# A two-layer centroid convolution on one core: alternating logits rounds with numerators and denominators, a reordered head, and centring on GpSimd

## The chip, the cores and the metric

The kernel runs on one core of a Trainium2 chip. The metric is the device time of one execution in microseconds. The program was run several times and the median is given; one more execution was profiled, and every view of the profile comes from that one. Engines are named as the profile names them: PE is TensorE's matmuls, PEld its weight loads, DVE is VectorE, ACT is ScalarE, POOL is GpSimd, SP is the queue of SyncE that issues most DMAs. "SPq" in a view is SP's queue.

## The reference

The input x has 16 images of 256 channels with 28 x 28 pixels, float32. The output is `x + f(gn(x))`, where `gn` normalizes each of 32 groups of 8 channels over its group and its pixels, and `f` is

```python
out = amm_conv3x3(v, centroids1, wsub1)      # v = gn(x)
out = relu(bn1(out))
out = amm_conv3x3(out, centroids2, wsub2)
out = bn2(out)
out = se_layer(out)                          # mean over pixels, two small layers, sigmoid gate
return relu(out + v)

def amm_conv3x3(x, centroids, w_sub):        # centroids [C, 16, 9], w_sub [C, 9, 256]
    p = 3x3 patches of x                     # per channel and pixel, 9 taps
    d = squared distance of p to each of the channel's 16 centroids
    attn = softmax(-d)                       # over the 16 centroids
    lut = centroids @ w_sub                  # per channel, [16, 256]
    return sum over channels and centroids of attn * lut
```

As `lut = centroids @ w_sub`, the result of a layer is also a product of `w_sub` with the softmax-weighted mean of the centroids, nine numbers per channel and pixel, and this is how the kernel computes it. The square of p is the same for all centroids of a channel and drops out of the softmax.

## The kernel before

**Tiles.** A layer of an image is cut into four blocks: half of the input channels (`hh`, 128 channels) by half of the pixels (`t`, 14 rows, N = 392 pixels), in the order `BLOCKS = ((0, 0), (0, 1), (1, 1), (1, 0))`. For each block the kernel

- gathers the nine taps of each channel from a padded image in HBM into a patch tile `pt` (`patches`, six DMAs for each half p of the block, issue lines L335 and L339; the source is called `home`);
- multiplies them by the centroids: `logits` (L349) of four groups mm = 0 to 3, each of 32 channels. One round of a group is 16 matmuls on 32 x 32 tiles of the array into four PSUM banks; two halves p = 0 (mm 0, 1) and p = 1 (mm 2, 3) take one patch tile each;
- takes exponentials of the four banks on ScalarE (`exps`, L361) into `e`;
- computes the ninth numerator and the denominators, summed over all four groups (`num_b`, L410, two banks "nb"), splits and joins them on ScalarE and VectorE (`split_b` L421 and L423, `join_b` L430 and L433), and takes the reciprocal (L436);
- computes the other numerators (`num_a`, L396, two banks "na" per group). Groups 0 and 1 are copied out by ScalarE (`copy_a`, L464) and multiplied by the reciprocal on GpSimd (`scale_q`, L459); groups 2 and 3 are multiplied on VectorE as they leave PSUM (`scale_a`, L470). `spread` (L447, L451) brings the reciprocals to the right partitions.

The fp32 matmuls take two passes, so that one round of logits shows as 32 matmul instructions.

**Products.** The four blocks of an image form a 2 x 2 by 2 x 2 product with `w_sub`, done with seven products in place of eight; sums of operands are made on GpSimd (`mix`, L485 and L487). Each product is nine matmuls on the full array (`product`, L478, into a bank "acc"), and VectorE and ScalarE put the results together (`acc_copy`, `acc_add` L515, `norm_out` L533).

**Layer 2, hh = 0.** These blocks are "wide": the logits of mm = 0 may be too large for a plain exponential. They are copied (`wide_copy`, L367), turned and their maximum taken on VectorE (`wide_turn`, L372 and L375), the maximum subtracted on GpSimd (`wide_sub`, L381), turned back (`wide_back`, L385) and only then exponentiated (`wide_exp`, L389).

**Order.** The order of work is written out by hand. `at(cluster, sub, function, ...)` files a step under a cluster number and a position inside it; at the end all steps are emitted sorted by (cluster, sub), and every engine, and SP's queue of DMAs, runs its instructions in the order of emission. An image takes eight clusters, a block two: in cluster g (even) its mm 0 and 1 go, in g + 1 (odd) mm 2 and 3; in cluster g + 2 its denominators and the numerators of mm 0 and 1, in g + 3 the numerators of mm 2 and 3. So an even cluster holds on TensorE: two rounds of logits, `num_b` and two `num_a` of the block before, and a product; an odd cluster two rounds of logits, two `num_a` and a product. Images start every eight clusters, layer 2 follows layer 1 at cluster 128; 256 clusters carry logits.

**PSUM.** All banks come from one ring of eight (`p_ring`), which hands a freed bank to the next request. A round of logits takes four, `num_b` two, a `num_a` two, a product one.

**Patches.** There are two patch tiles (`NPT = 2`), so the patches for cluster c + 2 can be issued only when the logits of cluster c have read the tile. `patches` stands at position 0.5 of cluster c, and the staging loads for layer 2's weights at position 0.6.

**Weights of layer 2.** During clusters 8 to 80 the kernel ranks input channels of layer 2 and reorders its weights accordingly: loads into a staging tile (`h0_load` L633, `codes_load` L641, `sub_load` L651), scatters to HBM by GpSimd's DMAs, and then centring: `prep_wd2` squares a third of the centroid table (`center_sq`, L251), `prep_wd3` has TensorE sum the squares (`center_add`, L256) and adds them, `prep_wd4` subtracts means and stores. The staging tile is single.

**Head.** Before the first cluster the first image is normalized (`gn_stats`, `gn_mean`, `gn_var`, `gn_apply` for its two channel halves), written to HBM, the patch tiles are set to one, and the centroid tables of layer 1 are centred.

Of the kernel before, what the change touches and what calls it, by code (L numbers as in the profile page):

```python
# [17 lines left out]
P = 128  # L18
# [7 lines left out]
K = 16  # L26
# [10 lines left out]
NPT = 2  # L37
# [30 lines left out]
def kernel(  # L68
# [20 lines left out]
    nc = tc.nc  # L89
    B, C, _ = x.shape  # L90
    NB = C // P
# [115 lines left out]
    kbias = kst[:, 16:48]  # L207
# [40 lines left out]

    def center_sq(wf, c0, w):
        sq = rpool.tile([P, N], F32, tag="r", name="sq")  # L250
        nc.vector.tensor_mul(sq[:, :w], wf[:, c0 : c0 + w], wf[:, c0 : c0 + w])  # L251
        return sq
# [5 lines left out]

    def center_mean(wf, n):
        g = wf.rearrange("p (g k) -> p g k", k=K)  # L260
        nc.vector.tensor_reduce(cst[:, : n // K], g, axis=AX.X, op=ALU.add)
        nc.vector.tensor_scalar_mul(cst[:, : n // K], cst[:, : n // K], 1.0 / K)
        nc.vector.tensor_sub(g, g, cst[:, : n // K].unsqueeze(2).to_broadcast([P, n // K, K]))

# [410 lines left out]
    def prep_wd2(part):  # L675
        pw["sq"] = center_sq(pw["st"][:, 512:1536], 384 * part, min(384, 1024 - 384 * part))

# [3 lines left out]
    def prep_wd4():  # L681
        st = pw.pop("st")
        center_mean(st[:, 512:1536], 1024)
        f = st[:, 512:1536].rearrange("p (g n) -> p g n", n=32)
        nc.vector.tensor_sub(f, f, kbias.unsqueeze(1).to_broadcast([P, 32, 32]))
        nc.sync.dma_start(d_wd[1], st[:, 512:1536])
# [147 lines left out]
    def at(cl, sub, f, *a, **kw):  # L834
        jobs.setdefault((cl, sub), []).append((f, a, kw))
# [20 lines left out]
    for j, u in enumerate(blocks):  # L856
        g = 2 * j
        u["w"] = j
        wide = u["l"] == 1 and u["hh"] == 0
        for p in range(2):  # L860
            u["pt", p] = pts[p]
            at(g + p - NPT, 0.5, patches, u, p, nc.gpsimd if g + p < 5 else None)
            for q in range(2):
                mm = 2 * p + q
                at(g + p, 0.1 + 0.1 * q, logits, u, mm)
                if wide and mm == 0:
                    at(g, 0.12, wide_copy, u, mm)
                    at(g, 0.9, wide_turn, u, mm)
                    at(g, 0.95, wide_sub, u, mm)
                    at(g + 1, 0.3, wide_back, u, mm)  # L870
                    at(g + 1, 0.9, wide_exp, u, mm)
                else:
                    at(g + p, 0.12 + 0.1 * q, exps, u, mm)
        at(g + 2, 1.3, num_b, u)
        at(g + 2, 1.4, split_b, u)
        at(g + 2, 1.5, join_b, u)
        at(g + 2, 1.6, recip_dve, u)
        at(g + 2, 1.7, spread, u, 4)
        at(g + 2, 1.71, scale_q, u, 4)
        for mm in range(2):  # L880
            at(g + 2, 1.35, num_a, u, mm)
            at(g + 2, 1.45, copy_a, u, mm)
            at(g + 3, 1.8, spread, u, mm)
            at(g + 3, 1.8, scale_q, u, mm)
        for mm in range(2, 4):
            at(*((g + 2, 1.8) if mm == 2 else (g + 3, 0.05)), spread, u, mm)
            at(g + 3, 1.0, num_a, u, mm)
            at(g + 3, 1.1, scale_a, u, mm)

    for l in range(2):  # L890
        for b in range(B):
# [3 lines left out]
            for c, (w, r, ks) in PRODUCTS.items():  # L895
                at(g + c, 2.0, product, (n, c), us[r], w, ks)
            for mm in (4, 2, 3, 0, 1):
# [4 lines left out]
            c11, c12, c21, c22 = (0, 0), (0, 1), (1, 0), (1, 1)  # L902
            at(g + 6, 0.0, acc_copy, l, b, c11, (n, 5))
            at(g + 7, 0.0, acc_copy, l, b, None, (n, 6))
# [13 lines left out]
            if l == 0:  # L918
# [8 lines left out]
                if b + 1 < B:  # L927
                    at(g + (-1 if b else 2), 2.6, load_x, b + 1)
                    for q in range(NB):
                        at(g + (1 + 2 * q if b else 4), 0.3, gn_stats, b + 1, q)  # L930
                    at(g + 4, 1.05 if b else 1.96, gn_mean, b + 1)
                    at(g + 4, 1.33 if b else 1.97, gn_var, b + 1)
                    for q in range(NB):
                        at(g + 5, 0.9, gn_apply, b + 1, q)
                        at(g + 5, 1.9, to_home1, b + 1, q)
            else:
# [18 lines left out]

    at(1, 0.6, load_w, 0, "A11")
    at(3, 0.6, load_w, 0, "S3")
    at(3, 0.6, load_w, 0, "A22")
    at(6, 0.6, load_w, 0, "A12")
# [23 lines left out]
    for part in range(3):  # L983
        at(43 + 2 * part, 1.9, prep_wd2, part)
        at(44 + 2 * part, 1.05, prep_wd3, part)
    at(51, 0.3, prep_wd4)
    at(52, 0.6, prep_cw0)
# [18 lines left out]

    for k in range(NB):
        gn_stats(0, k)
        gn_mean(0, k, 1)
        gn_var(0, k, 1)  # L1010
        gn_apply(0, k)
        if k == 0:
            for i in range(2):
                to_home1(0, 0, i)
            nc.vector.memset(pts[0], 1.0)
            nc.gpsimd.memset(pts[1], 1.0)
    for hh in range(2):
        center(wts["wd", hh].rearrange("p a b c -> p (a b c)"), 512)
    at(-0.5, 0.7, to_home1, 0, 1)
    at(0, 1.95, setup_bn)  # L1020
    for t in hpads:
# [159 lines left out]
```

## Time and profile before

| | value |
|---|---|
| median of 3 runs | 2773.7 us (2772.71 to 2774.86) |
| the profiled execution | 2760.28 us |
| its span, first to last instruction | 2758.7 us |
| mean granted clock of TensorE | 0.987 |
| PE busy | 2674.9 us (97%) |
| PEld busy | 1297.7 us (47%) |
| DVE busy | 1732.6 us (63%) |
| ACT busy | 1454.4 us (53%) |
| POOL busy | 2066.8 us (75%) |

A row of the timeline or of the groups reads: start, busy time, engine, line, operation, output tile <- input tiles, shape, number of instructions, and in brackets the engine's idle time before it with the tile and line that released it. In the row of slices each digit is the busy share of a fortieth of the span in tenths. A row of the waits names who waited, for whom, the total in us, how often, and the longest. The profiled execution is 13.4 us shorter than the median of the timed runs, so sums made on the profile are carried over as differences.

### The profile page before, as it was taken

The page shows a single profiled execution, that of the slowest core. Times are in us where ns is not written, and L with a number is a line of the kernel's source. Part 1 is how long each engine was busy: PE and PEld are TensorE (multiplying, and loading weights), DVE is VectorE, ACT ScalarE, POOL GpSimd, SP SyncE. Part 2 cuts the span into 40 slices and gives each one's busy share as a digit, 9 for nine tenths or more (in the row PEclk, how much of TensorE's full clock was granted, in tenths as well). Part 3 has the DMA queues.
Part 4 walks back from the last instruction along what each step waited for, and adds up shares of the span by engine and source line. Part 5 has one row for each costly group of instructions (what it writes and reads, how often), then busy time and mean ns, then how long its engine had stood idle before and what let it go on. Part 6 is the DMA issues. An engine that isn't in the chain of part 4 may idle for free. (4 is left out here: it accounts for less than half of the span.)

```text
span 2758.7 us, 87946 instructions
## 1 busy us (share of the span) xinstructions
PE 2674.9 (97%) x37076; PEld 1297.7 (47%) x37076; DVE 1732.6 (63%) x3950; ACT 1454.4 (53%) x3277; POOL 2066.8 (75%) x1420
## 2 busy tenths in 40 slices
PE   5989999799999999999999999999999999999997
PEld 2444444344444444444444444444444444444443
DVE  5765555765555565565576766676766666766664
ACT  4444455445455445455455466656566656556653
POOL 4756787738877767766678777888877788877787
PEclk9999999999999999999999999999999999999998
DMA  9665677546677656666585455445555545555541
GB/s 202 149 135 136 165 191 184 146 107 158 154 189 189 157 128 151 158 160 150 117 183 122 105 123 122 111 104 114 114 123 123 115 104 113 116 117 123 117 105 47
DMA packets 223025, 374.51 MB, mean 136 GB/s; under 512 B 30152, under 2 KB 193336, under 8 KB 222624
## 3 DMA queue, kind: packets, MB, share of 16 engines
q1 hardware_dynamic: 215392, 334.50, 53.8%
q0 software_dynamic: 7232, 34.30, 3.6%
q8 instruction: 296, 4.85, 0.8%
q14 instruction: 105, 0.86, 0.1%
HBM read 288.91 MB, written 79.80 MB: 134 GB/s over the span
## 5 line engine op out<-in xcount | busy, mean ns | idle before, releaser
L361 ACT ACTIVATE e<-lg 128x392 f32<-128x392 f32 x1920 | 777.7, 530 | 822.7 <-PE lg L349 821.7
L487 POOL TENSOR_TENSOR qp<-qp,qp 128x784 f32<-128x784 f32 x512 | 938.2, 1862 | 41.8 <-DVE qp L470 41.8
L478 PE MATMUL acc<-qp,w_S 128*128 128x392 f32 x2048 | 709.0, 497 | 5.3 <-POOL qp L487 5.2
L459 POOL TENSOR_TENSOR qp<-qp,rb 128x784 f32<-128x784 f32 x256 | 473.0, 1869 | 253.6 <-DVE rb L451 253.6
L349 PE MATMUL lg<-pt,wd 32*32 32x392 f32 x16384 | 533.5, 503 | 28.8 <-DVE half_sum L515 17.3
L451 DVE STREAM_SHUFFLE rb<-r 128x392 f32<-128x392 f32 x1024 | 550.8, 605 | 0.0
L478 PEld LDWEIGHTS acc<-qp,w_S 128*128 128x128 f32 x2048 | 388.5, 191 | 296.7 <-POOL qp L487 10.9
L478 PE MATMUL acc<-qp,w_A 128*128 128x392 f32 x1536 | 521.3, 493 | 0.0
L396 PE MATMUL na<-e,cwa 64*32 64x392 f32 x8192 | 412.1, 498 | 10.0 <-issue 9.8
L430 DVE SCALAR_TENSOR_TENSOR r<-nb,kst,r 128x392 f32<-128x392 f32 x128 | 79.8, 624 | 517.5 <-ACT r L421 510.6
L478 PEld LDWEIGHTS acc<-qp,w_A 128*128 128x128 f32 x1536 | 292.5, 190 | 213.1
L410 PE MATMUL nb<-e,cwb 64*32 64x392 f32 x8192 | 372.2, 497 | 0.0
L349 PEld LDWEIGHTS lg<-pt,wd 32*32 32x32 f32 x16384 | 230.9, 103 | 282.8 <-issue 179.6
L436 DVE RECIPROCAL r<-r 128x392 f32<-128x392 f32 x128 | 331.9, 2593 | 0.0
L459 POOL TENSOR_TENSOR qo<-qo,rb 128x392 f32<-128x392 f32 x128 | 131.1, 1024 | 220.3 <-DVE rb L447 220.2
L470 DVE TENSOR_TENSOR qp<-na,rb 128x392 f32<-128x392 f32 x512 | 252.4, 555 | 56.1 <-PE na L396 53.1
L396 PEld LDWEIGHTS na<-e,cwa 64*32 64x32 f32 x8192 | 145.2, 106 | 234.6 <-ACT e L361 123.5
L410 PEld LDWEIGHTS nb<-e,cwb 64*32 64x32 f32 x8192 | 146.2, 107 | 209.2 <-issue 126.5
L464 ACT COPY qp<-na 128x392 f32<-128x392 f32 x512 | 211.8, 512 | 10.9 <-PE na L396 10.8
L421 ACT ACTIVATE r<-nb,kst 128x392 f32<-128x392 f32 x128 | 87.5, 684 | 102.3 <-PE nb L410 99.8
L367 ACT COPY e<-lg 128x392 f32<-128x392 f32 x128 | 52.9, 500 | 152.9 <-PE lg L349 152.9
L485 POOL TENSOR_TENSOR qo<-qo,qo 128x392 f32<-128x392 f32 x128 | 130.8, 1022 | 2.2
(143 smaller groups left out, 1778.1 us busy)
## 6 DMA issues: line engine op xcount, KB each, us to landing
pt<-home SPq DMA_DIRECT2D x768, 209.0 KB
pt<-home SPq DMA_DIRECT2D x753, 104.5 KB
home<-xpad SPq DMA_DIRECT2D x31, 899.0 KB
xt<-in_x SPq DMA_DIRECT2D x30, 784.0 KB
out_dram<-y SPq DMA_DIRECT2D x32, 392.0 KB
w_S<-d_wS SPq DMA_DIRECT2D x4, 576.0 KB
st<-in_wsub SPq DMA_DIRECT2D x4, 512.0 KB
st<-d_wa SPq DMA_DIRECT2D x16, 128.0 KB
```

Source lines behind the costliest of these rows:

```text
L349: nc.tensor.matmul(bk[32 * c : 32 * c + 32, :N].rearrange("p (r w) -> p r w", w=W), lhsT=wts["wd", u["hh"]][32 * i : 32 * i + 32, mm, c, : ...
L361: nc.scalar.activation(eg[:, i, :], bk[:, :N], AF.Exp, scale=2.0)
L396: nc.tensor.matmul(bs[r][32 * i : 32 * i + 32, :N], lhsT=wts["cwa", u["hh"]][64 * r : 64 * r + 64, mm, i, :], rhs=es[64 * r : 64 * r + 64, ...
L410: nc.tensor.matmul(bs[r][32 * i : 32 * i + 32, :N], lhsT=wts["cwb", u["hh"]][64 * r : 64 * r + 64, mm, i, :], rhs=es[64 * r : 64 * r + 64, ...
L436: nc.vector.reciprocal(u["r"], u["r"])
L451: nc.vector.stream_shuffle(rb[:, r, :], u["r"], mask_of(2 * mm + r))
L459: nc.gpsimd.tensor_tensor(q, q, u.pop(("rb", mm)), ALU.mult)
L464: nc.scalar.copy(u["q", 2 * mm + r], bk[:, :N])
L470: nc.vector.tensor_mul(u["q", 2 * mm + r], bk[:, :N], rb[:, r, :])
L478: nc.tensor.matmul(accs[key][:, :N], lhsT=wl[w][:, k, :], rhs=us["q", k], start=first and n == 0, stop=last and n == len(ks) - 1,)
L485: nc.gpsimd.tensor_tensor(out_u["q", 8], in0["q", 8], in1["q", 8], ALU.subtract)
L487: nc.gpsimd.tensor_tensor(pair(out_u, mm), pair(in0, mm), pair(in1, mm), ALU.subtract)
```

## The change

The change has four parts.

1. **Rounds.** In an even cluster the second round of logits (mm 1) goes from position 0.2 to 1.32, behind `num_b`, and its `exps` to 1.42, behind `split_b`; the two `num_a` go to 1.45, so that `join_b` at 1.5 is emitted behind them. In an odd cluster the second round (mm 3) goes to 1.12, behind the numerators of mm 2, and the numerators of mm 3 to 1.2.
2. **Patches.** All patch DMAs go from 0.5 to 1.6 of their cluster, and so behind the loads that stand at 0.6 and ahead of those at 1.65 and later.
3. **Centring of layer 2.** The squares (`prep_wd2`), the subtraction of the means and that of `kbias` (`prep_wd4`) go from VectorE to GpSimd, and `prep_wd4` from position 0.3 to 1.9 of cluster 51.
4. **Head.** The patch tile is set to one in two pieces; the first centroid table is centred between the normalizations of the two channel halves, the second one in cluster 0; some loads and the work on the second image get other positions; the first image's first product is made in cluster 4 in place of 5.

```diff
--- before.py
+++ after.py
@@ -246,9 +246,9 @@
 
     cst = const.tile([P, 64], F32, name="cst")
 
-    def center_sq(wf, c0, w):
+    def center_sq(wf, c0, w, eng=None):
         sq = rpool.tile([P, N], F32, tag="r", name="sq")
-        nc.vector.tensor_mul(sq[:, :w], wf[:, c0 : c0 + w], wf[:, c0 : c0 + w])
+        (eng or nc.vector).tensor_mul(sq[:, :w], wf[:, c0 : c0 + w], wf[:, c0 : c0 + w])
         return sq
 
     def center_add(wf, c0, w, sq):
@@ -256,11 +256,11 @@
         nc.tensor.matmul(ps[:, :w], lhsT=nhalf_sb, rhs=sq[:, :w], start=True, stop=True)
         nc.vector.tensor_add(wf[:, c0 : c0 + w], wf[:, c0 : c0 + w], ps[:, :w])
 
-    def center_mean(wf, n):
+    def center_mean(wf, n, eng=None):
         g = wf.rearrange("p (g k) -> p g k", k=K)
         nc.vector.tensor_reduce(cst[:, : n // K], g, axis=AX.X, op=ALU.add)
         nc.vector.tensor_scalar_mul(cst[:, : n // K], cst[:, : n // K], 1.0 / K)
-        nc.vector.tensor_sub(g, g, cst[:, : n // K].unsqueeze(2).to_broadcast([P, n // K, K]))
+        (eng or nc.vector).tensor_sub(g, g, cst[:, : n // K].unsqueeze(2).to_broadcast([P, n // K, K]))
 
     def center(wf, n):
         for c0 in range(0, n, 256):
@@ -673,16 +673,16 @@
             )
 
     def prep_wd2(part):
-        pw["sq"] = center_sq(pw["st"][:, 512:1536], 384 * part, min(384, 1024 - 384 * part))
+        pw["sq"] = center_sq(pw["st"][:, 512:1536], 384 * part, min(384, 1024 - 384 * part), nc.gpsimd)
 
     def prep_wd3(part):
         center_add(pw["st"][:, 512:1536], 384 * part, min(384, 1024 - 384 * part), pw["sq"])
 
     def prep_wd4():
         st = pw.pop("st")
-        center_mean(st[:, 512:1536], 1024)
+        center_mean(st[:, 512:1536], 1024, nc.gpsimd)
         f = st[:, 512:1536].rearrange("p (g n) -> p g n", n=32)
-        nc.vector.tensor_sub(f, f, kbias.unsqueeze(1).to_broadcast([P, 32, 32]))
+        nc.gpsimd.tensor_sub(f, f, kbias.unsqueeze(1).to_broadcast([P, 32, 32]))
         nc.sync.dma_start(d_wd[1], st[:, 512:1536])
 
     def prep_cw0():
@@ -859,10 +859,10 @@
         wide = u["l"] == 1 and u["hh"] == 0
         for p in range(2):
             u["pt", p] = pts[p]
-            at(g + p - NPT, 0.5, patches, u, p, nc.gpsimd if g + p < 5 else None)
+            at(g + p - NPT, 1.6, patches, u, p, nc.gpsimd if g + p < 5 else None)
             for q in range(2):
                 mm = 2 * p + q
-                at(g + p, 0.1 + 0.1 * q, logits, u, mm)
+                at(g + p, (0.1, (1.32, 1.12)[p])[q], logits, u, mm)
                 if wide and mm == 0:
                     at(g, 0.12, wide_copy, u, mm)
                     at(g, 0.9, wide_turn, u, mm)
@@ -870,7 +870,7 @@
                     at(g + 1, 0.3, wide_back, u, mm)
                     at(g + 1, 0.9, wide_exp, u, mm)
                 else:
-                    at(g + p, 0.12 + 0.1 * q, exps, u, mm)
+                    at(g + p, (0.12, (1.42, 1.14)[p])[q], exps, u, mm)
         at(g + 2, 1.3, num_b, u)
         at(g + 2, 1.4, split_b, u)
         at(g + 2, 1.5, join_b, u)
@@ -878,14 +878,14 @@
         at(g + 2, 1.7, spread, u, 4)
         at(g + 2, 1.71, scale_q, u, 4)
         for mm in range(2):
-            at(g + 2, 1.35, num_a, u, mm)
-            at(g + 2, 1.45, copy_a, u, mm)
+            at(g + 2, 1.45, num_a, u, mm)
+            at(g + 2, 1.46, copy_a, u, mm)
             at(g + 3, 1.8, spread, u, mm)
             at(g + 3, 1.8, scale_q, u, mm)
         for mm in range(2, 4):
             at(*((g + 2, 1.8) if mm == 2 else (g + 3, 0.05)), spread, u, mm)
-            at(g + 3, 1.0, num_a, u, mm)
-            at(g + 3, 1.1, scale_a, u, mm)
+            at(g + 3, 1.0 if mm == 2 else 1.2, num_a, u, mm)
+            at(g + 3, 1.1 if mm == 2 else 1.25, scale_a, u, mm)
 
     for l in range(2):
         for b in range(B):
@@ -893,14 +893,14 @@
             g = 8 * n
             us = blocks[4 * n : 4 * n + 4]
             for c, (w, r, ks) in PRODUCTS.items():
-                at(g + c, 2.0, product, (n, c), us[r], w, ks)
+                at(g + c - (c == 5 and n == 0), 2.0, product, (n, c), us[r], w, ks)
             for mm in (4, 2, 3, 0, 1):
                 at(g + 5, 2.5, mix, us[0], mm, us[1], us[0])
                 at(g + 7, 2.5 if mm < 2 else 1.75, mix, us[1], mm, us[2], us[1])
                 at(*((g + 7, 2.6) if n < B - 1 else (g + 8, 1.0)), mix, us[0], mm, us[2], us[0])
                 at(g + 10, 1.0, mix, us[0], mm, us[0], us[3])
             c11, c12, c21, c22 = (0, 0), (0, 1), (1, 0), (1, 1)
-            at(g + 6, 0.0, acc_copy, l, b, c11, (n, 5))
+            at(g + (6 if n else 5), 0.0, acc_copy, l, b, c11, (n, 5))
             at(g + 7, 0.0, acc_copy, l, b, None, (n, 6))
             at(g + 8, 0.0, acc_add, l, b, None, (n, 7))
             at(g + 9, 0.0, acc_add, l, b, c21, (n, 8), c11)
@@ -925,14 +925,14 @@
                         for r in range(2):
                             at(g + 12 + o + (o and r), (0.5, 2.9)[r] if o == 0 else (2.4, 2.9)[r], to_home2, b, o, r)
                 if b + 1 < B:
-                    at(g + (-1 if b else 2), 2.6, load_x, b + 1)
+                    at(*((g - 1, 2.6) if b else (2, 1.65)), load_x, b + 1)
                     for q in range(NB):
                         at(g + (1 + 2 * q if b else 4), 0.3, gn_stats, b + 1, q)
-                    at(g + 4, 1.05 if b else 1.96, gn_mean, b + 1)
-                    at(g + 4, 1.33 if b else 1.97, gn_var, b + 1)
+                    at(g + 4, 1.05 if b else 2.1, gn_mean, b + 1)
+                    at(g + 4, 1.33 if b else 2.2, gn_var, b + 1)
                     for q in range(NB):
-                        at(g + 5, 0.9, gn_apply, b + 1, q)
-                        at(g + 5, 1.9, to_home1, b + 1, q)
+                        at(g + 5, 0.9 if b else 0.3, gn_apply, b + 1, q)
+                        at(g + 5, 1.9 if b or q else 0.9, to_home1, b + 1, q)
             else:
                 last = b == B - 1
                 at(*((g + 11, 0.6) if last else (g + 13, 2.6)), load_x, b, last)
@@ -953,9 +953,9 @@
                     at(g + 11, 0.95, flags)
                     at(g + 12, 2.9, flag_sum)
 
-    at(1, 0.6, load_w, 0, "A11")
-    at(3, 0.6, load_w, 0, "S3")
-    at(3, 0.6, load_w, 0, "A22")
+    at(1, 1.65, load_w, 0, "A11")
+    at(3, 1.65, load_w, 0, "S3")
+    at(3, 1.65, load_w, 0, "A22")
     at(6, 0.6, load_w, 0, "A12")
     for c, m in ((5, "S1"), (7, "S2"), (8, "S4"), (6, "S3")):
         at(c, 1.96, combine, m)
@@ -983,7 +983,7 @@
     for part in range(3):
         at(43 + 2 * part, 1.9, prep_wd2, part)
         at(44 + 2 * part, 1.05, prep_wd3, part)
-    at(51, 0.3, prep_wd4)
+    at(51, 1.9, prep_wd4)
     at(52, 0.6, prep_cw0)
     at(53, 1.9, prep_cwa)
     for part in range(4):
@@ -1004,20 +1004,26 @@
     at(g + 4, 0.6, load_w, 1, "A12")
     at(g + 5, 0.6, load_w, 1, "A22")
 
-    for k in range(NB):
+    def norm0(k):
         gn_stats(0, k)
         gn_mean(0, k, 1)
         gn_var(0, k, 1)
         gn_apply(0, k)
-        if k == 0:
-            for i in range(2):
-                to_home1(0, 0, i)
-            nc.vector.memset(pts[0], 1.0)
-            nc.gpsimd.memset(pts[1], 1.0)
-    for hh in range(2):
+
+    def center_wd(hh):
         center(wts["wd", hh].rearrange("p a b c -> p (a b c)"), 512)
+
+    nc.vector.memset(pts[0][:, :4], 1.0)
+    norm0(0)
+    for i in range(2):
+        to_home1(0, 0, i)
+    nc.vector.memset(pts[0][:, 4:], 1.0)
+    nc.gpsimd.memset(pts[1], 1.0)
+    center_wd(0)
+    norm0(1)
+    at(0, 1.95, center_wd, 1)
     at(-0.5, 0.7, to_home1, 0, 1)
-    at(0, 1.95, setup_bn)
+    at(0, 1.96, setup_bn)
     for t in hpads:
         at(1, 1.95, nc.gpsimd.memset, t, 0.0)
```

## The prediction

> **What bounds the kernel now.** I read the busy row first, then the slices, then TensorE's busy time in stretches.
>
> ```profile
> PE 2674.9 (97%) x37076; PEld 1297.7 (47%) x37076; DVE 1732.6 (63%) x3950; ACT 1454.4 (53%) x3277; POOL 2066.8 (75%) x1420
> PE   5989999799999999999999999999999999999997
> 2006.30:2088.70 82.40, 82.40 (x1179) 40.35 (x1192) 55.54 (x120) 48.90 (x112) 66.84 (x41) 1.00 0.51 115
> ```
>
> TensorE sets the time, with about 84 us of idle, nearly all before 800 us and in the tail. The third line is one layer-2 image (start:end, length, then PE, PEld, DVE, ACT, POOL, clock, DMA): no gap. A TensorE wait added to a cluster is thus lost in full; a gain must shorten TensorE's own runs. The timeline shows them (start, length):
>
> ```profile
> 2006.30 2.03 PE L349 MATMUL lg<-pt,wd 32*32 32x392 f32 x64
> 2008.25 2.86 PE L410 MATMUL nb<-e,cwb 64*32 64x392 f32 x64
> 2010.91 1.52 PE L396 MATMUL na<-e,cwa 64*32 64x392 f32 x32
> 2012.37 0.93 PE L478 MATMUL acc<-qo,w_A 128*128 128x392 f32 x2
> 2018.49 2.02 PE L349 MATMUL lg<-pt,wd 32*32 32x392 f32 x64
> 2020.44 1.64 PE L396 MATMUL na<-e,cwa 64*32 64x392 f32 x32
> 2022.01 0.93 PE L478 MATMUL acc<-qo,w_A 128*128 128x392 f32 x2
> ```
>
> From start to start an even cluster spends 2012.37 − 2006.30 = 6.07 us ahead of its product, an odd one 3.52. In the single records the first logits round of a pair takes 0.68 us and the second 1.27: weight loads run ahead in the first, then trickle.
>
> ```profile
> 2046.83 2.86 PE L410 MATMUL nb<-e,cwb 64*32 64x392 f32 x64
> 2047.35 1.72 ACT L361 ACTIVATE e<-lg 128x392 f32<-128x392 f32 x4
> 2049.79 0.68 ACT L421 ACTIVATE r<-nb,kst 128x392 f32<-128x392 f32 x1 [0.72 <-PE nb L410]
> 2050.37 0.67 ACT L423 ACTIVATE qo<-nb,kst 128x392 f32<-128x392 f32 x1
> 2047.52 1.81 DVE L372 STREAM_TRANSPOSE z<-e 128x1568 f32<-128x1568 f32 x1 [1.53 <-ACT e L367]
> 2049.37 1.79 DVE L375 TENSOR_REDUCE mx<-z 128x98 f32<-128x1568 f32 x1
> 2051.61 0.63 DVE L433 SCALAR_TENSOR_TENSOR qo<-nb,kst,qo 128x392 f32<-128x392 f32 x1
> ```
>
> This is a wide cluster (layer 2, hh = 0). The exponentials run under the denominators, and VectorE's long turn ahead of `join_b` costs TensorE nothing: its product began at 2050.94, before `join_b` ended at 2052.24.
>
> ```profile
> SPq L641 <- DMA home<-st,col: 15.3, 1, 15.3
> SPq L633 <- DMA home<-st,col: 9.7, 1, 9.7
> SPq L651 <- DMA d_wa<-st,col: 24.2, 3, 11.2
> PE lg L349 <- DVE half_sum L515: 17.3, 2, 15.4
> 535.52 16.73 DVE L251 TENSOR_TENSOR sq<-st 128x256 f32<-128x256 f32 x1
> ```
>
> (Waited for in total, times, longest.) The staging loads of layer 2's weights hold SP's queue for 10 to 15 us at a time, at present behind the patches of their cluster. And one squaring took 16.73 us on VectorE (0.42 in the head).
>
> **What the Trainium skill says.** "PSUM — Partial Sum Buffer", Engine vs sequencer instructions: ScalarE's and VectorE's queues are strict FIFO and matmuls start in program order; the rows agree (L361, then L421). "TensorE: Matmul & The Clock Gate", Architectural detail: TensorE's queue of 64 can pull weight loads ahead; the 0.68/1.27 pattern agrees, 33 loads standing at the front of 64. "SBUF — State Buffer", Who interferes with whom: a VectorE port pair shared with GpSimd is locked exclusively; the 16.73 us agree, GpSimd running back to back from 532.98 to 552.
>
> **Rounds, even clusters (128).** Now: logits mm0, denominators (`num_b`), logits mm1, numerators, product. No instruction goes. Separate rounds I take at 0.68 plus a restart of about 0.2 = 0.87 each (estimate); denominators 2.66 plus a drain of 0.14 = 2.80. Without waits: 0.87 + 2.80 + 0.87 + 1.45 = 5.99, a gain of 0.08. But the eight PSUM banks circulate. In the order of the built program, ScalarE now runs exps mm0, the two splits, exps mm1; the second bank of `num_a` mm1 waits for the first exp of mm1, and the product for the second `join_b`. From the end of the denominators: split starts +0.14, two at a pace of 0.56, exp starts +1.26, ends +1.76, TensorE resumes +1.87 (handover 0.11, as elsewhere); seven of eight numerator steps and the last bank's drain remain, 0.82: product at +2.69. So 0.87 + 2.80 + 2.69 = 6.36 against 6.07: **+0.29**, times 128 = **+36** (bounds −10 to +55: without the wait −0.08, with 0.15 more +0.44). Queued behind the wait is the product, and behind it everything.
>
> **Odd clusters (128).** Logits mm2, numerators mm2, logits mm3, numerators mm3. mm3's last banks wait for exps mm2, then the product waits for the first half of `scale_a` mm2. ScalarE's exps, the first 0.93 after the logits' start and one each 0.39, pace the cluster: my sum is 3.53 against 3.52, **0** (bounds −25 to +15: unpaced it would be 3.3 to 3.4; 0.12 more if `scale_a` comes late).
>
> **Wide clusters (32 of each).** `join_b` sits behind L372 and L375. By the trace its second half ends 52.24 − 44.85 = 7.39 after the logits' start; the product can start at 7.5, not 6.36: 1.14 × 32 = **+36**. In the odd ones `wide_back` (1.79) delays `scale_a` to 60.39 + 0.56 − 57.07 = 3.9: 0.46 × 32 = **+15**. ScalarE's `finish_relu` and normalizing (2.2 us) ahead of the splits in one even cluster an image: 0.82 × 15 = **+12**; GroupNorm statistics in odd layer-1 clusters: **+3**. Together +66 (bounds +20 to +85). Steady part: **+102**.
>
> **Patches moved from 0.5 to 1.6.** Each is six DMAs, 3.6 us of issue on SP, landing up to 5.5–9.8 us later, wanted two clusters on, about 17 us: alone free. But the loads at 0.6 now stand ahead of them on SP. `h0_load(22)` was issued at 283.58; patches behind it land at about 292, logits(24) began at 280.53: +11.5. By the same sum: `codes_load` at 310.64 +5, `sub_load` at 367.60 +7, 390.05 +0.7, 449.90 +7, `prep_wd0` +2.7, `prep_cw0` behind `prep_wd4` +5. Sum **+39** (10 to 55: a load's own release may move). Each loss is the landing minus the start of logits two clusters later in the trace of before; after cluster 80 no such load waits. In return GpSimd-held late patches near 286 to 298 no longer stop TensorE: **−5**.
>
> **Centring on GpSimd.** Three squarings (0.6 to 0.9 us, scaled from GpSimd's 1862 ns for 784 columns) and the two 1024-wide subtractions (about 2.43 each) add 7 us to a GpSimd at 75%, by itself covered. What goes is the 16.73 us lock: 15.4 us of wait and 4–5 after it, 20 in all. What comes: the `sqp` matmul (L256), in front of the numerators and product of its cluster, waits for GpSimd to come to the squaring behind its mixes: by GpSimd's rows near the three places 1.8, 0.6 and 4.5, about 7 in all. `prep_wd4` from 0.3 to 1.9 of cluster 51 only delays its own store. **−13** (−20 to −5).
>
> **Head.** VectorE now does a small memset, norm 0, the rest of the memset, one centring, and only then norm 1; the first patch DMAs on GpSimd are queued behind norm 1's rsqrt, which moves from about 15 to 19–21 us: first logits at about 28.7 instead of 24.7, +4 (nothing to +8, if the later patches follow). SP's `load_w` and `load_x` go from 0.6 and 2.6 to 1.65, on either side of the patches there: their data is wanted clusters later, nothing. The other centring at (0, 1.95) and norm 1's two `to_home1` are hidden behind patches on the way. Product 5 moved to cluster 4 fills the wait of 5.17 us that the `gnp` matmul (L303) has at 63.19 for the GroupNorm's mean: −5 (0 if the mean is late again after it). `acc_copy` one cluster sooner frees its bank sooner: nothing. **0** (−6 to +8).
>
> **Sum:** 102 + 39 − 5 − 13 + 0 = +123, of which I take **+117**, since a cluster late by patches has its exps and joins done. The profiled execution is 2760.3 (span 2758.7); its 13.4 us distance to the median 2773.7 I keep: 2773.7 + 117 ≈ **2890**. 0.2% (5.5 us) is about what a measurement can tell.
>
> **Rivals.**
> A, loads release early: the rounds cost 102, SP's loads nothing; 102 − 5 − 13 = +84, 2858. For it: some of the loads wait on work that the delay itself does not hold up. Against: landings of 9.7 to 15.3 us are measured.
> B, waits cost more: 0.15 more for each even cluster (+19) and odd ones at their bound (+15): 123 + 34 = +157, 2931. For it: the handovers are taken at their shortest.
> C, only SP and centring count, the rounds' waits being made up by shorter rounds: 39 − 5 − 13 = +21, 2795. Against: the wide clusters' joins end at 7.39 by the trace.
> D, **faster**: mm1's first exp arrives before the numerators want it and a round is 0.68, not 0.87: 0.2 to 0.43 us per pair of clusters × 128 = 26 to 55, and 13 from centring; 2720. For it: the slow second round is 1.27. It decides at +1.57 after the denominators' end for that exp, where my chain gives +1.76, and at a `join_b` before +2.3, which wide clusters break.
> E, the change does not do what it says: logits still go at the old pace, and SP's losses cancel the centring: within 5 us.
>
> **How the numbers follow.** Forecast 0.52, A 0.18, B 0.13, C 0.08, D 0.07, E 0.02. Range 2812 to 2938: the forecast's own range is 2865 to 2915 (20 us for SP, 15 for the even clusters); it reaches on to A and B, and leaves out C, D and E, 0.17. Faster 0.07, same 0.02, slower 0.91.
>
> **What would show it.** Right: L396 with idle released by ACT L361, L478 by DVE L433 for about 1 us in 32 clusters, L470 releasing L478; SP waiting at L633, L641, L651 and TensorE's wait for pt growing from 8.8 us to some 40; no VectorE squaring above 1 us. Wrong: a wide cluster still at 6.1 us to its product (C or D), a logits round of 0.68 on both sides of the denominators with no wait (D), or no TensorE wait for pt (A).

## The result, and the profile after

The changed kernel takes 2889.1 us (median of 4 runs, 2883.1 to 2897.5) against 2774.3 us before on the same chip, a ratio of 1.0416 with a 95% interval of 1.0383 to 1.0448: slower by 115 us. The forecast was 2890. The profiled execution of the changed kernel has a span of 2892.5 us, 133.8 more than the profiled one before. The two profiles are not quite alike: that of the changed kernel (2894.03 us) is one of its four timed runs, while that of before (2760.28 us) lies under all four timed runs of before on this chip (2772.7 to 2776.4) and close to what before takes on the chips of the experiments (2756 to 2758). So some 14 us of the 133.8 may come from the chip or the session and not from the change. Sums over the traces have to reach about 134, sums over medians about 115, and the ratio is the fairer of the two.

The page of the changed kernel, busy row, slices of PE, and three groups (busy us, mean ns, then idle before and who ended it); the last line is the group L396 in the kernel before:

```profile
PE 2730.4 (94%) x37076; PEld 1259.2 (44%) x37076; DVE 1729.8 (60%) x3945; ACT 1464.3 (51%) x3278; POOL 2073.7 (72%) x1425
PE   5799889999999999999999999999999999999997
L349 PE MATMUL lg<-pt,wd 32*32 32x392 f32 x16384 | 514.0, 505 | 66.6 <-DMA pt<-home 49.0
L396 PE MATMUL na<-e,cwa 64*32 64x392 f32 x8192 | 483.1, 502 | 11.4 <-ACT qo L423 9.9
L410 PE MATMUL nb<-e,cwb 64*32 64x392 f32 x8192 | 391.0, 502 | 0.0
L396 PE MATMUL na<-e,cwa 64*32 64x392 f32 x8192 | 412.1, 498 | 10.0 <-issue 9.8
```

TensorE's idle time went from 84 to 162 us, but that is only 78 of the 134. The other 56 appear as busy time: the same 8192 matmuls of `num_a` are busy for 483.1 us where they were 412.1, with the same mean of about 500 ns. Records of about 500 ns overlap inside a run, so a wait shorter than that is not idle time in this view; it stretches the run (p6_split_dve below takes such a wait out of one run). Not all of the 71 us is waiting: in odd clusters the numerators now go in two runs of about 0.95 us where they were one of 1.64, while the logits lost 19 us of busy time (533.5 to 514.0). The slices hardly show any of it.

The timeline of a wide even cluster (192), TensorE first and VectorE below:

```profile
2138.61 0.94 PE L349 MATMUL lg<-pt,wd 32*32 32x392 f32 x32
2139.48 2.94 PE L410 MATMUL nb<-e,cwb 64*32 64x392 f32 x64
2142.36 0.95 PE L349 MATMUL lg<-pt,wd 32*32 32x392 f32 x32
2143.24 1.78 PE L396 MATMUL na<-e,cwa 64*32 64x392 f32 x32
2146.14 0.90 PE L478 MATMUL acc<-qo,w_S 128*128 128x392 f32 x2 [1.11 <-DVE qo L433]
2141.28 1.81 DVE L372 STREAM_TRANSPOSE z<-e 128x1568 f32<-128x1568 f32 x1 [1.99 <-ACT e L367]
2143.12 1.78 DVE L375 TENSOR_REDUCE mx<-z 128x98 f32<-128x1568 f32 x1
2145.37 0.62 DVE L433 SCALAR_TENSOR_TENSOR qo<-nb,kst,qo 128x392 f32<-128x392 f32 x1
```

This is the wait that the prediction named. The product starts 2146.14 − 2138.61 = 7.53 us after the logits (7.5 in the prediction, 6.09 before): VectorE's turn and maximum stand ahead of `join_b`, and the product now waits for `join_b`.

A plain even cluster of layer 2 (206), TensorE and then ScalarE:

```profile
2297.18 0.94 PE L349 MATMUL lg<-pt,wd 32*32 32x392 f32 x32
2301.81 1.78 PE L396 MATMUL na<-e,cwa 64*32 64x392 f32 x32
2303.52 0.93 PE L478 MATMUL acc<-qo,w_S 128*128 128x392 f32 x2
2301.59 0.67 ACT L423 ACTIVATE qo<-nb,kst 128x392 f32<-128x392 f32 x1
2302.16 1.66 ACT L361 ACTIVATE e<-lg 128x392 f32<-128x392 f32 x4
```

Logits to product is 6.34 us (6.36 predicted, 6.07 before). No idle time is printed. The prediction's wait for the first exponential (it starts at 2302.16) would lie inside the 1.78 us of the numerators; p6_split_dve tests whether it does.

The waits of TensorE and of SP's queue (us in total, times, longest); the first line is from the kernel before:

```profile
PE lg L349 <- DMA pt<-home: 8.8, 3, 6.6
PE lg L349 <- DMA pt<-home: 49.0, 9, 10.8
PE acc L478 <- DVE qo L433: 33.3, 32, 1.1
PE lg L349 <- DVE half_sum L515: 12.7, 1, 12.7
SPq L651 <- DMA d_wa<-st,col: 49.3, 4, 15.7
SPq L633 <- DMA home<-st,col: 17.6, 1, 17.6
SPq L641 <- DMA home<-st,col: 16.2, 1, 16.2
```

TensorE's waits for patches went from 8.8 to 49.0 us, and exactly 32 products wait for `join_b`, 1.04 us each. The wait for `half_sum` was not foreseen: the 15.4 us wait for `half_sum` of before is gone, and another wait of 12.7 us for the same tile has come, near 111 us. VectorE's timeline says why (first line), beside GpSimd's last mixes of that stretch; below them the same places in the kernel before:

```profile
90.40 20.70 DVE L188 TENSOR_TENSOR w_S<-w_S,w_A 128x1152 f32<-128x1152 f32 x1
102.69 7.20 POOL L487 TENSOR_TENSOR qp<-qp,qp 128x784 f32<-128x784 f32 x4
92.55 2.06 DVE L188 TENSOR_TENSOR w_S<-w_S,w_A 128x1152 f32<-128x1152 f32 x1
106.58 2.81 DVE L188 TENSOR_TENSOR w_S<-w_A,w_S 128x1152 f32<-128x1152 f32 x1
102.72 8.40 POOL L487 TENSOR_TENSOR qp<-qp,qp 128x784 f32<-128x784 f32 x4
```

A subtraction that took 2.06 us before (`combine` of S2, in cluster 7) now takes 20.70. It was not edited. In the kernel before, GpSimd ran without a break from 89.72 to 112.11, and both combines (S2 and, at 106.58, S4) were still served inside that run; GpSimd's four mixes took 8.40 us there for 7.20 in the changed kernel, so that GpSimd waited for VectorE. In the changed kernel it is VectorE that waits, until GpSimd's run ends at 109.89.

For the parts I used the trace as a ruler: the time from the first logits of one cluster to those of the next, changed minus before, for all 256 clusters. In most clusters of layer 2 the differences repeat to 0.03 us from image to image. Ahead of cluster 81, where patches and weights disturb the pace, single steps differ by up to 3.4 us even between kernels that are the same up to there. The table has medians over the images from cluster 81 on (us; columns are clusters 0 to 7 of an image):

```
                      0     1     2     3     4     5     6     7
changed, layer 1    0.27  0.02  0.14  0.02  0.90  0.02  0.56  0.54
changed, layer 2    1.40  0.44  1.28  0.50  1.43  0.02  0.28  0.02
p4_rounds, layer 1  0.28  0.02  0.15  0.02  0.14  0.02  0.28  0.08
p4_rounds, layer 2  1.41  0.43  1.28  0.50  1.43  0.02  0.28  0.02
```

### The profile page after: what moved, and what is told of

It reads as the page before. It is cut to its first block, busy times and chain, and to the rows that moved or that the text cites. A ratio compares the mean times of both kernels' runs of the same rounds, so it can differ in the third digit from the quotient of the medians.

```text
span 2892.5 us, 87961 instructions
## 1 busy us (share of the span) xinstructions
PE 2730.4 (94%) x37076; PEld 1259.2 (44%) x37076; DVE 1729.8 (60%) x3945; ACT 1464.3 (51%) x3278; POOL 2073.7 (72%) x1425
## 5 line engine op out<-in xcount | busy, mean ns | idle before, releaser
L361 ACT ACTIVATE e<-lg 128x392 f32<-128x392 f32 x1920 | 800.0, 506 | 885.8 <-PE lg L349 879.2
L478 PE MATMUL acc<-qp,w_S 128*128 128x392 f32 x2048 | 703.7, 494 | 0.9 <-POOL qp L487 0.9
L349 PE MATMUL lg<-pt,wd 32*32 32x392 f32 x16384 | 514.0, 505 | 66.6 <-DMA pt<-home 49.0
L478 PE MATMUL acc<-qp,w_A 128*128 128x392 f32 x1536 | 521.2, 492 | 0.0
L478 PEld LDWEIGHTS acc<-qp,w_S 128*128 128x128 f32 x2048 | 386.5, 190 | 297.7 <-issue 14.3
L396 PE MATMUL na<-e,cwa 64*32 64x392 f32 x8192 | 483.1, 502 | 11.4 <-ACT qo L423 9.9
L410 PE MATMUL nb<-e,cwb 64*32 64x392 f32 x8192 | 391.0, 502 | 0.0
L478 PEld LDWEIGHTS acc<-qp,w_A 128*128 128x128 f32 x1536 | 291.8, 190 | 213.8
L349 PEld LDWEIGHTS lg<-pt,wd 32*32 32x32 f32 x16384 | 136.0, 103 | 366.4 <-issue 250.6
L410 PEld LDWEIGHTS nb<-e,cwb 64*32 64x32 f32 x8192 | 208.7, 108 | 167.9 <-issue 94.0
L396 PEld LDWEIGHTS na<-e,cwa 64*32 64x32 f32 x8192 | 142.4, 105 | 316.7 <-ACT e L361 78.4
L478 PE MATMUL acc<-qo,w_S 128*128 128x392 f32 x256 | 118.0, 543 | 39.4 <-DVE qo L433 33.3
L515 DVE TENSOR_TENSOR hpad<-acc,hpad 128x392 f32<-128x392 f32 x80 | 43.9, 565 | 172.4 <-PE acc L478 135.8
```

The source lines that it names most:

```text
L349: nc.tensor.matmul(bk[32 * c : 32 * c + 32, :N].rearrange("p (r w) -> p r w", w=W), lhsT=wts["wd", u["hh"]][32 * i : 32 * i + 32, mm, c, : ...
L361: nc.scalar.activation(eg[:, i, :], bk[:, :N], AF.Exp, scale=2.0)
L396: nc.tensor.matmul(bs[r][32 * i : 32 * i + 32, :N], lhsT=wts["cwa", u["hh"]][64 * r : 64 * r + 64, mm, i, :], rhs=es[64 * r : 64 * r + 64, ...
L410: nc.tensor.matmul(bs[r][32 * i : 32 * i + 32, :N], lhsT=wts["cwb", u["hh"]][64 * r : 64 * r + 64, mm, i, :], rhs=es[64 * r : 64 * r + 64, ...
L478: nc.tensor.matmul(accs[key][:, :N], lhsT=wl[w][:, k, :], rhs=us["q", k], start=first and n == 0, stop=last and n == len(ks) - 1,)
```

## The experiments

Ratios are to the kernel before, on the same chip, with 95% intervals. The median of before was 2756 to 2758 us on these chips, against 2774.3 beside the result; the changed kernel was not run again beside them.

**The four parts, one at a time.** The rounds cannot be tried with the patches at 0.5: the patches for cluster c + 2 would overwrite the tile that the second round, now at 1.32, has still to read. So the rounds run has the patches at 1.6 with the staging loads put behind them.

p1_patches, the patches alone:

```diff
-            at(g + p - NPT, 0.5, patches, ...)
+            at(g + p - NPT, 1.6, patches, ...)
```

> The kernel before with the patches alone at 1.6. Theory (staging loads ahead of the patches on SP): +25 to +35 us, in steps at the logits of clusters 24, 32 and 40 (about +11, +7, +7) and a gain near cluster 25; nothing after cluster 80. Rival (the later position itself makes patches late): every cluster from 16 on gets longer, well over +50 us. Rival (the loads are released early enough): within 5 us.

Measured: 1.0129 (1.0109 to 1.0148), +35.6 us, and 32.2 in the trace. The trace gives +12.3 at the start of logits 24, +9.3 at 32 and +7.1 at 40, −2.2 at 25, steps of 2.2 to 2.5 at 33, 41, 65 and 80, and 0.00 in nearly every cluster from 81 on. TensorE's and SP's timelines:

```profile
280.12 0.33 SPq L633 DMA_DIRECT2D st<-d_h  x1
291.53 3.35 PE L349 MATMUL lg<-pt,wd 32*32 32x392 f32 x64 [12.21 <-DMA pt<-home]
```

The load is issued at 280.12, the patches only then, and logits(24) wait 12.21 us for them. The position as such costs nothing; a queue that waits ahead of it does.

p2_centre, the centring of layer 2 alone (the `eng` arguments of the change and `prep_wd4` at 1.9):

> The kernel before with the centring of layer 2 alone on GpSimd. Theory (the 16.73 us squaring was held by GpSimd's run of work): -13 to -18 us, a step of about -15 at clusters 48 to 49, the squarings under 1 us on GpSimd, and under 3 us of new waits at L256. Rival (the lock goes over to another VectorE instruction, or TensorE waits for GpSimd's queue instead): -5 to +5 us.

Measured: 0.9951 (0.9935 to 0.9968), −12.6 us, just short of the range expected; −13.3 at cluster 48. The squarings as the trace lists them (shortest/median/longest ns):

```profile
L251 POOL TENSOR_TENSOR sq<-st x3: 605/819/826, 493.6 to 537.2; 128x384 f32<-128x384 f32 x2, 128x256 f32<-128x256 f32 x1
```

The new wait of TensorE at L256 is one of 3.3 us, a little over the 3 expected. The theory holds.

p3_head, the head's part alone:

> The kernel before with the head's part alone. Theory of the prediction (first logits +3 to +4, given back by the product in cluster 4): -6 to +5 us. Rival (the head's new order by itself puts the combine L188 of cluster 8 under GpSimd's run of mixes, 20.7 us in the changed kernel against 2.06): +5 to +12 us with that long instruction in the trace; if it is absent here, the rounds or patches brought it about.

Measured: 1.0050 (1.0027 to 1.0072), +13.8 us by the ratio. The first logits come 4.3 later; with the product gone from it cluster 5 is 5.4 shorter, while clusters 4 and 6 take 2.3 of that back; by cluster 8 the balance is +0.6, near the 0 predicted. Then one step of +18.2, VectorE first and then TensorE's waits:

```profile
93.60 18.35 DVE L188 TENSOR_TENSOR w_S<-w_S,w_A 128x1152 f32<-128x1152 f32 x1
PE lg L349 <- DVE half_sum L515: 34.1, 2, 18.8
```

The head's new alignment is enough to bring the long combine about; neither rounds nor patches are needed. Of the four runs behind the ratio three lie 17 to 20 us above before and one 5; only one was traced, so it is open whether the combine is held in every execution.

p4_rounds, the rounds, the patches at 1.6, and the staging loads behind them:

```diff
+            rounds and patches as in the change
-        at(20 + 2 * o, 0.6, h0_load, o)
+        at(20 + 2 * o, 1.65, h0_load, o)
... (likewise code_load, codes_load, sub_load, prep_wd0, prep_cw0, sums_load)
```

> The kernel before with the rounds and the patches at 1.6, and the staging loads put behind the patches (1.65), centring and head as before. Theory (waits inside the clusters: first exp of mm 1, join_b, scale_a): about +105 us (95 to 120): +0.28 in a plain even cluster, +1.4 and +1.3 in the wide ones, +0.44 to +0.50 in wide odd ones, 0.02 in other odd ones. Rival (the loss is late patches): under +20 us once the loads are behind them. Rival (the alternation itself gains and the loss comes from head and loads): below the time before.

Measured: 1.0322 (1.0304 to 1.0340), +88 us, with the steps of the table above. TensorE's waits:

```profile
PE acc L478 <- DVE qo L433: 33.3, 32, 1.1
PE lg L349 <- DMA pt<-home: 17.6, 5, 5.8
```

The wait for `join_b` is that of the changed kernel to the last digit, and that for patches is down to a third. The loss of the steady state is inside the clusters. It was below the expected 95 to 120: layer 1 loses 1.0 us an image, where the changed kernel's row of the table adds up to 2.5. Of the +86.8 in the traces, 79.8 lie in layer 2.

**p5_wide_late**, VectorE's turn taken from ahead of `join_b`:

```diff
-                    at(g, 0.9, wide_turn, u, mm)
-                    at(g, 0.95, wide_sub, u, mm)
-                    at(g + 1, 0.3, wide_back, u, mm)
-                    at(g + 1, 0.9, wide_exp, u, mm)
+                    at(g, 1.75, wide_turn, u, mm)
+                    at(g, 1.76, wide_sub, u, mm)
+                    at(g + 1, 1.3, wide_back, u, mm)
+                    at(g + 1, 1.9, wide_exp, u, mm)
... (finish_norm and finish_gate from 0.9 to 1.4, since they share the tile)
```

> p4_rounds with wide_turn behind join_b (1.75), wide_sub after it, wide_back at 1.3 behind scale_a, wide_exp at 1.9 (and finish_norm at 1.4, behind the tile they share). Theory (the product of a wide cluster waits for join_b behind VectorE's turn): the wide even steps fall from +1.41 and +1.28 to about +0.28 and +0.15, the odd ones from +0.44 and +0.50 to 0.02: -48 us against p4_rounds, so about +40 against before. Rival (the turn is not what join_b waits for): as p4_rounds, +88. Rival (the exponential now comes too late for the denominators): a new wait of TensorE ahead of L410, 1 to 3 us in each of 32 clusters, +70 to +130.

Measured: 1.0302 (1.0277 to 1.0328), +85 us. Against p4_rounds the wide even steps fell by 1.15 and 1.04 and the wide odd ones by 0.42 and 0.48: the theory's numbers. But cluster 4 of each image grew by 2.7 to 4.4 us and took it all back. TensorE and ScalarE there:

```profile
2225.77 2.87 PE L410 MATMUL nb<-e,cwb 64*32 64x392 f32 x64 [1.82 <-ACT e L389]
2224.22 1.49 ACT L389 ACTIVATE e<-e 128x1568 f32<-128x1568 f32 x1
```

That is the rival's wait, in one cluster of eight and by my own edit: I had put `finish_norm` and `finish_gate`, 3.7 us on ScalarE, ahead of the wide exponential. The cause of the wide steps is shown, a version without them is not.

**p6_split_dve**, the second half of `split_b` on VectorE:

```diff
-        nc.scalar.activation(q, b0[:, :N], AF.Identity, bias=zero, scale=m_lo)
+        nc.vector.tensor_scalar(q, b0[:, :N], m_lo, None, op0=ALU.mult)
```

> p4_rounds with the second half of split_b on VectorE. Theory (the numerators of mm 1 wait for the first exp of mm 1, which stands behind two splits on ScalarE): that exp starts 0.56 earlier, its end falls before TensorE wants the bank; plain even clusters go from +0.28 to about -0.08, the ones at +0.14 likewise; wide clusters get up to 0.55 longer (VectorE has one instruction more ahead of join_b); in all -10 to -25 us against p4_rounds. Rival (another wait is behind the +0.28, the pace of the rounds or join_b): plain even clusters stay at +0.28 or grow.

Measured: 1.0311 (1.0288 to 1.0335), +87 us. Plain even clusters went from +0.28 to +0.11, cluster 2 of layer 1 from +0.15 to −0.02, and cluster 4 of layer 2 fell by 0.28. The wide ones grew by 0.21 and 0.27, and clusters 4 and 7 of layer 1 from 0.14 and 0.08 to 0.22 and 0.28; the sum is nil. TensorE and ScalarE in cluster 206:

```profile
2249.92 0.94 PE L349 MATMUL lg<-pt,wd 32*32 32x392 f32 x32
2253.67 0.95 PE L349 MATMUL lg<-pt,wd 32*32 32x392 f32 x32
2254.55 1.62 PE L396 MATMUL na<-e,cwa 64*32 64x392 f32 x32
2256.10 0.93 PE L478 MATMUL acc<-qo,w_S 128*128 128x392 f32 x2
2254.66 1.67 ACT L361 ACTIVATE e<-lg 128x392 f32<-128x392 f32 x4 [0.22 <-PE lg L349]
```

The exp is no longer behind the splits: ScalarE waits 0.22 us for the logits, so it starts as early as it can. Still the cluster takes 2256.10 − 2249.92 = 6.18 us to its product against 6.07 before. So the wait behind the splits is 0.16 to 0.17 of the 0.28; the 0.11 that remains comes without it. In these clusters alternating gains nothing even with that wait gone. From start to start the two logits rounds together are 0.20 us shorter than before (0.87 and 0.88 for 1.95), the denominators 0.22 longer (2.88 for 2.66) and the numerators 0.09 longer (1.55 for 1.46).

**p7_no_head** (rounds, patches and centring) and **p11_prod5** (all but the first product's place and the steps moved with it) look for the layer-1 excess in clusters 4, 6 and 7.

> The changed kernel with the head as before (rounds, patches and centring only). In the changed kernel the layer-1 clusters with GroupNorm work and the two odd-numbered pairs after them are 0.9, 0.6 and 0.53 longer, in p4_rounds 0.14, 0.28 and 0.08. If the head's part brings that (by the PSUM banks that steps get): 0.14, 0.28, 0.08 here, and about +95 to +105 us in all. If it is the centring or the loads' place: 0.9, 0.6 and 0.53 here, and +110 to +120 us. The parts alone add up to +111 (35.6 - 12.6 + 88).

Measured: 1.0398 (1.0359 to 1.0437), +108 us; steps 0.13, 0.27 and 0.08. In the traces the excess goes with the head's part.

```diff
-                at(g + c - (c == 5 and n == 0), 2.0, product, (n, c), us[r], w, ks)
+                at(g + c, 2.0, product, (n, c), us[r], w, ks)
... (acc_copy, gn_mean, gn_var, gn_apply and to_home1 as before)
```

> The changed kernel with the first product back in cluster 5 (with acc_copy and the GroupNorm steps of the second image as before); the rest of the head, rounds, patches and centring as changed. In the changed kernel the layer-1 clusters 4, 6 and 7 of each image are 0.9, 0.6 and 0.53 longer, in p7_no_head 0.13, 0.27 and 0.08. If the product's place brings that on: 0.13, 0.27 and 0.08 here. If the rest of the head does: 0.9, 0.6, 0.53. The wait at cluster 8 for the held combine may come or go with the alignment of VectorE and GpSimd; 0 or 12 us.

Measured: 1.0402 (1.0382 to 1.0423), +109 us; steps 0.13, 0.28 and 0.08, and S2's combine takes 2.08 us. In the traces the excess goes with the place of one product in cluster 4 and the steps around it. That this is its cause is not shown. A rival stands untested: the excess may belong to the chip or the session of the result, where before takes 2774.3 us, and not to the change. The traces of the changed kernel and of p11_prod5 are 29.4 us apart, some 20 of them in layer 1 after cluster 16, but set against before on its own chip each is 1.0416 and 1.0402, about 4 us apart. The five runs that move the product without the rounds (p3, p8, p9, p10, p12) show 0.00 in these clusters, and p6_split_dve, with the product in its old place, shows 0.22 and 0.28 in two of the three. From cluster 16 to the end of layer 1 all four engines run the same instructions in the same order in both traces, so that nothing in the program's order explains it. What the traces do show is a pause inside a run of matmuls, for instance the second logits round of cluster 92, in the changed kernel and then in p4_rounds:

```profile
1061.74 1.79 PE L349 MATMUL lg<-pt,wd 32*32 32x392 f32 x32
```

```profile
1021.86 1.02 PE L349 MATMUL lg<-pt,wd 32*32 32x392 f32 x32
```

**p8_head_s4, p9_best, p10_head_s2, p12_best2**: the held combine, and a better version. p8 is head and centring with S4's combine on GpSimd:

```diff
-        nc.vector.tensor_tensor(wl[n], wl[a], wl[b], op)
+        (nc.gpsimd if n == "S4" else nc.vector).tensor_tensor(wl[n], wl[a], wl[b], op)
```

> The head's part and the centring, with the combine of S4 (L188, cluster 8) on GpSimd; rounds and patches as before. Theory (the 18.2 us step of p3_head at cluster 8 is a VectorE instruction with two SBUF inputs held by GpSimd's run of mixes): the step is under 3 us, the longest L188 on VectorE under 3 us, and the time is that of p2_centre or some us below: -10 to -17 us against before. Rival (TensorE waits there for something else, such as late patches or GpSimd itself): the step stays over 10 us, in all about 0.

Measured: 1.0018 (1.0001 to 1.0035), +3.5 us; the step at cluster 8 is still 17.7 above p2_centre, because I had moved the wrong combine. VectorE:

```profile
95.56 20.22 DVE L188 TENSOR_TENSOR w_S<-w_S,w_A 128x1152 f32<-128x1152 f32 x1
```

`w_S<-w_S,w_A` is S2 of cluster 7; S4 would read `w_S<-w_A,w_S`. p10 has "S2" in that line:

> As p8_head_s4, but with the combine that the trace shows held, S2 of cluster 7 (w_S<-w_S,w_A), on GpSimd; in p8 it still took 20.2 us on VectorE. Theory: the 17.7 us step at cluster 8 falls under 3 us; -10 to -16 us against before. Rival (half_sum L515, for which TensorE waited, is late for another reason): the step stays above 10 us, 0 to +7.

Measured: 0.9989 (0.9977 to 1.0001), −3.0 us, so no difference from before is settled. The step at cluster 8 is gone (−1.1), but cluster 9 has +9.4: S4, left on VectorE, now takes 12.4 us.

p9 is before with centring, the first product in cluster 4, and S2 on GpSimd; p12 has "S2" and "S4" there.

> The kernel before with the centring on GpSimd, the first product in cluster 4 (acc_copy in 5, GroupNorm steps of the second image as in the changed kernel), and the combine S2 of cluster 7 on GpSimd; rounds, patches and the rest of the head as before. Theory: the centring's -12.6 us and up to -5 of the 5.2 us wait at L303: -13 to -18 us against before. Rival (later waits of the head take the product's gain back): -10 to -13. Rival (GpSimd's 2.7 us for S2 delay its mixes and TensorE): above -8.

Measured: 0.9977 (0.9967 to 0.9987), −5.7 us, short of the theory's −13 to −18. Against p2_centre the trace is 3.2 us ahead at cluster 8; then S4 takes 12.2 us on VectorE, and cluster 9 loses 8.9.

> p9_best with the combine S4 of cluster 8 on GpSimd as well: in p9_best, S2 gone, S4 took 12.2 us on VectorE and clusters 8 to 10 lost 7.6 us on p2_centre. Theory (the lock passes to the next VectorE instruction with two SBUF inputs that stands beside GpSimd's run, and none is left): the step goes, -14 to -20 us against before. Rival (GpSimd, 2.6 us later for each combine, or another VectorE instruction, now holds TensorE): -4 to -10, no better than p2_centre.

Measured: 0.9969 (0.9959 to 0.9980), −9.0 us, not the −14 to −20 of the theory but what its rival said. The step of S4 is gone, and another VectorE instruction is held in its place (0.98 us before), in a cluster that is 7.1 us longer than before:

```profile
111.57 6.83 DVE L562 TENSOR_SCALAR c<-c 128x144 f32<-128x144 f32 x1
```

No try is clearly better than the centring alone. p2_centre, 0.9951 (0.9935 to 0.9968), is faster than both kernels.

## Why the prediction was right, and where it was not

The time, the sign and most terms held; two terms missed in opposite directions. Of the signs named for it, the waits of L478 for L433 in 32 clusters, those for the patches and those of SP came. Idle time of L396 released by L361 did not: 9.9 of its 11.4 us are released by the second split (L423), in 14 clusters.

- **Even clusters**, predicted +0.29: +0.28 in plain ones, but 0.14 in half of layer 1's (p4_rounds). Its inside was half wrong. I put 5.99 us for the cluster without the wait and 0.37 for the wait; p6 shows 6.18, and 0.16 to 0.17. A round at 0.87 to 0.88 was right; the denominators take 2.88 where I had 2.80, and the numerators 1.55 where I kept 1.45. The slow second round (1.27) was not saved: PEld's busy time fell by 95 us for logits (230.9 to 136.0) and rose by 62 for the denominators (146.2 to 208.7), so it seems that the trickle of weight loads moved into the run behind it.
- **Odd clusters**, predicted 0: 0.02.
- **Wide clusters**: even +36 predicted; 1.13 and 1.00 above a plain cluster, 16 times each, is 34. Odd +15: (0.44 + 0.50) × 16 = 15. p5 shows the cause. In the cluster with `finish_relu` +0.82 in 15 clusters was predicted, 1.15 in 14 measured. GroupNorm +3: about 1 in p4_rounds (0.08 in cluster 7). All rounds: 102 predicted, 86.8 in p4_rounds' trace; the term that was too large is layer 1, where I took 0.29 for each even cluster.
- **Patches and SP**, predicted +39 − 5: p1_patches +35.6. The three large loads cost what was worked out (12.3, 9.3 and 7.1 for 11.5, 7 and 7); the smaller ones at logits 26, 43 and 54 (5, 2.7 and 5) did not appear as losses, and the steps of 2.2 to 2.5 at 33, 41, 65 and 80, which the prediction did not have, made up for them.
- **Centring**, predicted −13: −12.6. The sum was luckier than its terms: the end of the long squaring was put at 20 us and gave 16.6 (13.3 gained at cluster 48, with a new wait of 3.3 inside it), and the new waits were put at 7 and came to 3.3.
- **Head**, predicted 0 with a bound of +8: +13.8. This is the step that failed. Its own terms were about right (first logits +4.3 for +4; cluster 5 −5.4 for −5, some 3 of it kept), but it treated "the 16.73 us lock" as a property of one squaring. It can befall other VectorE instructions that are issued inside a run of GpSimd's, though it need not: S2's combine stood inside such a run in the kernel before too and got through in 2.06 us. Shifting the head by some us decided against it. I had the mechanism from the Trainium skill ("SBUF — State Buffer", Who interferes with whom: a VectorE instruction with two inputs in SBUF contends with a GpSimd instruction that reads SBUF) and did not ask which other VectorE instructions a shift would expose. The trace agrees: the combine has two inputs in SBUF and took 20.70 us.
- **The sum**: in the traces the parts give 32.2 − 13.5 + 16.5 + 86.8 = 122, the whole change 133.8; by medians they give 35.6 − 12.6 + 13.8 + 88 = 125, the whole 115, with an interval of 106 to 124. So the parts fall short of the whole by one measure and exceed it by the other. In the traces the excess of layer 1 is part of the difference; its cause stays open, and it may be the chip's. That the forecast fell within 1 us of the median is partly luck: the rounds were put some 15 us too high and the head some 14 too low.

Of the rivals, A (loads released early) falls by p1_patches, C (rounds at nothing) by p4_rounds, and D (faster) by p6_split_dve: without the wait on which it was to hang, a plain alternating cluster is still 0.11 longer. B's extra waits in each cluster and E's standstill are not in the table of steps.

## What to carry to other kernels

When TensorE is never idle, look for what it will newly wait for in the circulating PSUM banks and in the order of the engine that frees them: a long VectorE instruction is free while nobody needs what stands behind it, and costs its full overhang once somebody does. A step moved behind another one on a queue inherits that one's wait, so price each wait ahead of the new place, not the place. And when VectorE is held behind GpSimd once, list the other instructions that can fall into it before moving anything by a few microseconds: here the same combine beside the same kind of run took 2 us or 20.

## What the runs showed of the hardware

- A VectorE instruction caught by GpSimd can wait for GpSimd's whole run of instructions, not for one: S2's combine (2.06 us before) took 18 to 21 us, and GpSimd's run beside it in the changed kernel was twelve instructions, ten of them about 1.83 us each, back to back from 89.93 to 109.89, with the combine issued at 90.40. "SBUF — State Buffer", Who interferes with whom, has whoever issues first keep the shared ports for the whole instruction while the other blocks; that alone would give a wait of one GpSimd instruction.
- It can also be served in between: in the kernel before the same two combines took 2.06 and 2.81 us inside a GpSimd run of 89.72 to 112.11, and the GpSimd instructions behind them 2.97 and 2.99 us where the others took about 1.86. What decides between the two is not shown.
- The instruction that was held in p12_best2 is a tensor_scalar with one input (6.83 us for 0.98). The same section counts tensor_scalar among those that can enter a mode that takes both ports, when its operands allow it. The 6.83 us fit that; no run tests whether it was in that mode.
- A wait shorter than a matmul's record counts as busy time of TensorE: in cluster 206 the run of numerators is 1.78 us with the wait behind the splits and 1.62 without (p6_split_dve), with no idle time printed in either. The group as a whole is busy for 71 us more, with 1.4 us more idle; how much of the 71 is waiting is not shown.
